# A cross-attention kernel: the last 128 columns of the next keys as 15 block products among the wide products with V

## The chip, the cores and the metric

The kernel runs on one core of a Trainium2 chip. Its time is the device time of one execution in microseconds; the figure before the change is the median of three runs, 932.97 us (932.73 to 934.45). A profile of one more execution (933.61 us) shows where that time goes.

## The reference

There are 16 batches of 100 queries with 640 channels (`x`) and a context of 722 rows with 384 channels, of which the last 4 rows are tokens (`ca`) and the first 718 the keys' rows (`enc`). Eight heads of 80 channels.

```
query = x @ Wq;  keyt = enc @ Wk;  valt = enc @ Wv
hs = mha(query, keyt, valt)                      # the main attention, over 718 rows
ca_q1 = (ca^T @ Wq_ca)[picked rows]              # the second attention:
ca_hs1 = mha(ca_q1, x, x)                        #   over x itself,
ca_hs2 = mha(ca_hs1 @ Wq, ca @ Wk_ca, ca @ Wv_ca)#   and then over the 4 tokens
out = (hs + ca_hs2) @ Wout + b_out + x
```

Everything is float32. `mha` is softmax(q k^T / sqrt(80)) v for each head.

## The kernel before

**Work of a batch.** The main loop runs over the batches `b`. In batch `b` TensorE does, in the order of the program: the scores of `b` in three groups (`scores`), two small products of the second attention (`z_ps`, `y_ps`), the values of `b` and the keys of `b + 1` block by block, alternating (`Values`, `Keys`), the last keys of `b + 1` (`last_keys`), the output projection of rows that are ready (`project`), in odd batches the queries of the next two batches (`queries`), the denominators of the softmax with a few output columns (`rests`, tile `r_ps`), and the wide products of the probabilities with V (`wides`, tile `a_ps`). Inside the loop each engine takes its instructions in the order in which they are written; nothing reorders them.

**Keys by blocks.** K^T is kept as `kT`, five chunks of 128 columns by three thirds of 240 rows. The first four chunks are made from 15 products of sums of blocks of the context (`a_form`) with sums of blocks of the weights (`wk_sb`, `weight_sums`), instead of 18 plain ones. `V_PLAN` and `K_PLAN` name for each product its PSUM bank (A to E), its number and the output block (third, half) to which the bank's content goes then. A bank carries a running sum: product after product is added to it, and after each the content is read out, the first time into an output block by an ACT copy, later by a DVE addition (`Blocks.go`). So a bank's next product has to wait until its content has been read. The fifth chunk, columns 512 to 639, is made plainly in `last_keys`: three thirds by three blocks of 128 input channels, nine products of 128 columns, weights in `wk4`, moved to `kT` by two ACT copies (L604).

**PSUM.** Eight banks in three pools: two pairs (`pair`), two single banks `psumk`, two single banks `psum1`. Score groups 0 and 2 use both pairs, group 1 the four single banks. `wides` and `rests` each take a `psum1`.

**Column halves.** In `wides` a head's 64 columns go to partitions 0 to 63 (even heads) or 64 to 127 (odd heads), so neighbouring products use different halves of the array's columns. Position `i * NH + h` counts these 48 products.

**Softmax.** The main maximum is taken on DVE (`larger`, then `Maximum`: transpose, reductions, spread, transpose back), followed by `subtract` on DVE and `exponential` on ACT for the three probability tiles `st`. The second attention has the same steps in `softmax1` (five steps of `Maximum` and the subtraction from `e1`) and `exponentials1` (L837). In batches 1 to 14 `softmax1` stands ahead of `project`, `exponentials1` ahead of `rests`. In batch 0 the first four steps stand ahead of `rests`, and the last step, the subtraction and the exponential stand at the batch's end.

**Quotients.** `divide` makes the inverse of the denominators (ACT L980, DVE L981 and L984), sends it through DRAM to `ratio` for later use by POOL (`place`), and finishes the last 128 output columns (ACT L997, DVE L999). It stands between `rests` and `wides`. `keep` copies the wide products out (ACT L1024).

Of the kernel before, what the change touches and what calls it, by code (L numbers as in the profile page):

```python
# [15 lines left out]
NH, D = 8, 80  # L16
# [123 lines left out]
K_PLAN = [V_PLAN[k] for k in (0, 1, 2, 3, 4, 6, 5, 7, 9, 11, 8, 12, 10, 13, 14)]  # L140


A_RAW = {(0, 0): 0, (0, 1): 1, (0, 2): 2, (1, 1): 3, (1, 2): 4, (2, 0): 5, (2, 1): 6}
A_REST = {(1, 0): 0, (2, 2): 1}
A_AT = {0: 0, 14: 1, 12: 2, 6: 3, 13: 4, 3: 5, 1: 6}
# [8 lines left out]
def kernel(  # L154
# [167 lines left out]
    ca_0 = small.tile([S, T, S], F32, tag="ca", name="ca_0", bufs=2)  # L322
# [164 lines left out]
    class Keys(Blocks):  # L487
# [9 lines left out]
        def product(self, at, f, first, last):  # L497
            for i in range(2):
                nc.tensor.matmul(  # L499
                    at[:, i * KT : (i + 1) * KT],  # L500
                    wk_sb[:, W_AT[f], i],
                    a_form(self.enc, f),
                    start=(first and i == 0),
                    stop=last,
                    skip_group_check=True,
                )

        def places(self, at, to):
            u, g = to
            yield (  # L510
                kT[:, : HC - 1].rearrange("p (i g) u k -> p i g u k", g=2)[:, :, g, u],
                at[:, : 2 * KT].rearrange("p (i k) -> p i k", i=2),
            )

    def enc_sums(enc):

# [71 lines left out]
    def chunk_keys(n, banks, weights, enc):  # L588
        copies = []
        for bank, thirds in zip(banks, ((0, 1), (2,))):  # L590
            for i, u in enumerate(thirds):
                for c in range(CC):
                    nc.tensor.matmul(  # L593
                        bank[:, i * KT : (i + 1) * KT],
                        weights[c],
                        a_raw(enc, u, c),
                        start=(i == 0 and c == 0),
                        stop=(c == CC - 1),
                        skip_group_check=True,
                    )  # L600
        for bank, thirds in zip(banks, ((0, 1), (2,))):
            w = len(thirds)
            copies.append(
                nc.scalar.copy(  # L604
                    kT[:, n, thirds[0] : thirds[0] + w],
                    bank[:, : w * KT].rearrange("p (u k) -> p u k", u=w),
                )
            )
        return copies

    def first_keys(enc):
        for n in range(HC - 1):
            banks = [psum(f"kT_ps_0_{n}_{k}") for k in range(2)]
            weights = [wk_sb[:, 2 * c + n % 2, n // 2] for c in range(CC)]
            copies = chunk_keys(n, banks, weights, enc)
        last_keys(0, enc)
        return copies[-1]

    def last_keys(b, enc):
        banks = pair(f"kT_ps_{b}")  # L620
        return chunk_keys(
            HC - 1,
            [banks[:, k] for k in range(2)],
            [wk4[:, c] for c in range(CC)],
            enc,
        )

# [110 lines left out]
    def load_m(b, behind=None):  # L738
        if b < 2:
            return lambda c: m_sb[c][:, b * HT : (b + 1) * HT]  # L740
        mb = small.tile([P, HC, HT], F32, tag="mb", name=f"mb_{b}", bufs=2)
# [19 lines left out]
    class Second:  # L761


        def __init__(self, b, xT, ca=None):
            self.b, self.xT = b, xT[:, b % 2]
            self.top = None

            self.ca = ca
            if ca is not None:
                return  # L770
            self.ca = small.tile([S, T, S], F32, tag="ca", name=f"ca_{b}", bufs=2)
# [167 lines left out]
    class Last:  # L939
# [36 lines left out]
        def divide(self, rests):  # L976

            b = self.b
            inverse = small.tile([P, S], F32, tag="inv", name=f"inv_{b}")
            nc.scalar.mul(inverse, rests[:, 0], qmask[:, 1:2])  # L980
            nc.vector.scalar_tensor_tensor(  # L981
                inverse, rests[:, 1], qmask[:, 0:1], inverse, ALU.mult, ALU.add
            )
# [12 lines left out]
            for to, cols in self.pieces():  # L996
                nc.scalar.mul(to[:, HC - 1], rests[:, 0, cols], qmask[:, 0:1])  # L997
            for to, cols in self.pieces():
                nc.vector.scalar_tensor_tensor(  # L999
                    to[:, HC - 1],  # L1000
# [159 lines left out]
    for c in range(HC):  # L1160
        w_ps = psum(f"w_ps_{c}")
        for cc in range(CC):
            nc.tensor.transpose(
                w_ps[:, cc * P : (cc + 1) * P], wkt_sb[:, c, cc * P : (cc + 1) * P], ident
            )
        act(
            wk_sb[:, c % 2 : 6 : 2, c // 2] if c < HC - 1 else wk4,
            w_ps[:, : CC * P].rearrange("p (a n) -> p a n", a=CC),
        )

    with tc.issue_after(summed.ins):
        for c in range(HC):
# [60 lines left out]
    for b in range(B):  # L1233
# [54 lines left out]
        if b == 0:  # L1288
# [29 lines left out]
        elif b + 1 < B:  # L1318
# [43 lines left out]
            second_next, enc_next = loads()  # L1362
            subtract(2)
            exponential(2)
            last_keys(b + 1, enc)
# [55 lines left out]
        if b == B - 2:  # L1421
            room = enc_tile("spare").rearrange("p f k -> p (f k)")
            spare.extend(room[:, i * H : (i + 1) * H] for i in range(2))
        mine.divide(rests)
        if b == B - 1:
            last.project((1,), True)
        wides = psum1(f"a_ps_{b}")[:, : 4 * S].rearrange("p (c q) -> p c q", c=4)
        for i in range(len(KC)):
            for h in range(NH):
                e = h % 2  # L1430
                nc.tensor.matmul(  # L1431
                    wides[64 * e : 64 * e + 64, h // 2],
                    slot(i, h, FIRST[e], 64),
# [66 lines left out]
```

## Time and profile before

| | |
|---|---|
| median of three runs | 932.97 us |
| the profiled execution | 933.61 us, span 931.9 us |
| TensorE busy | 923.7 us, 99% |
| DVE, ACT, POOL busy | 650.8, 375.4, 573.3 us |
| last keys (L593), all batches | 288 records at 128x240 with `wk4`, 144 products |
| wide products (L1431) | 1536 records, 768 products |

[...] In the timeline rows the first number is the start, the second the time from the first start to the last end; a matmul's recorded end lies behind the start of the next group, since products are pipelined. So lengths of TensorE's stages are best read as differences of starts. A releaser in brackets names what ended an engine's idle time.

### The profile page before, as it was taken

How to read it: one execution, taken by the hardware profiler on the slowest of the kernel's cores; microseconds unless marked ns; L12 is line 12 of the kernel's file. 1: busy time of each engine (PE TensorE's matmuls, PEld its weight loads, DVE VectorE, ACT ScalarE, POOL GpSimd, SP SyncE). 2: the span in 40 equal slices, each digit the busy share in tenths (PEclk: the TensorE clock that was granted, in tenths of full speed). 3: DMA queues.
4: the chain of work that ended last, by engine and by line, in shares of the span. 5: the costliest groups of instructions: out<-in, count | busy, mean ns of one | idle time of the engine just before them, and what ended most of it. 6: DMA issues, size and time to landing. Idle time of an engine off the chain costs nothing.

```text
span 931.9 us, 26041 instructions
## 1 busy us (share of the span) xinstructions
PE 923.7 (99%) x11183; PEld 784.3 (84%) x11183; DVE 650.8 (70%) x1087; ACT 375.4 (40%) x649; POOL 573.3 (62%) x622
## 2 busy tenths in 40 slices
PE   9999999999999999999999999999999999999998
PEld 6997879788897888988788887987889888897865
DVE  3848894886919678495955959578592876939583
ACT  2234534434334344533425434344532444434350
POOL 5649857576645865467682666756665566556444
PEclk9999999999999999999999999999999999999999
DMA  8712262051400504132131411314131050401212
GB/s 258 241 39 67 54 129 72 20 145 29 108 26 23 144 12 109 29 83 74 35 106 30 112 45 42 76 25 130 44 98 36 19 146 15 107 14 50 63 52 64
DMA packets 68667, 69.16 MB, mean 74 GB/s; under 512 B 26056, under 2 KB 62344, under 8 KB 68552
## 3 DMA queue, kind: packets, MB, share of 16 engines
q1 hardware_dynamic: 67224, 66.18, 26.9%
q8 instruction: 88, 1.44, 0.7%
q10 hardware_dynamic: 864, 0.98, 0.3%
q0 software_dynamic: 464, 0.34, 0.1%
q14 instruction: 27, 0.22, 0.1%
HBM read 61.81 MB, written 8.94 MB: 76 GB/s over the span
## 4 chain that ended last, share of the span: by engine, by line
PE 96%; DVE 2%; DMA 1%; issue 0%; ACT 0%; POOL 0%; SPq 0%; DVEq 0%; ACTq 0%
PE s_ps L643 12%; PE v_psA L468 10%; PE v_psB L468 8%; PE kT_ps L593 8%; PE k_psA L499 7%; PE q_ps L569 7%; PE a_ps L1431 7%; PE o_ps L1061 7%; PE k_psB L499 6%; PE r_ps L1413 4%; PE v_psC L468 3%; PE k_psC L499 3%; PE v_ps L409 2%; PE y_ps L782 2%; PE v_psD L468 2%; PE v_psE L468 2%
## 5 line engine op out<-in xcount | busy, mean ns | idle before, releaser
L817 POOL TENSOR_TENSOR e<-ca,g 100x800 f32<-100x800 f32 x64 | 99.4, 1564 | 156.8 <-DVE most L1263 140.4
L534 POOL TENSOR_TENSOR enc<-enc 128x240 f32<-128x240 f32 x135 | 96.5, 725 | 21.6 <-DMA enc<-in_enct 14.6
L468 PE MATMUL v_psA<-wv_sb,enc 128*120 128x320 f32 x352 | 109.6, 434 | 0.2 <-ACT st L671 0.2
L923 POOL TENSOR_TENSOR hs<-pb,vaT 128x500 f32<-128x500 f32 x64 | 73.0, 1150 | 53.7 <-DMA pb<-wide_d 51.2
L643 PE MATMUL s_ps<-qp,kT 32*120 32x100 f32 x3072 | 97.9, 263 | 0.0
L643 PEld LDWEIGHTS s_ps<-qp,kT 32*120 32x120 f32 x3072 | 95.0, 180 | 2.1 <-issue 0.2
L824 POOL TENSOR_TENSOR e<-e,e 100x800 f32<-100x800 f32 x48 | 90.6, 1887 | 3.8
L468 PE MATMUL v_psB<-wv_sb,enc 128*120 128x320 f32 x296 | 91.9, 433 | 0.0
L499 PE MATMUL k_psA<-enc,wk_sb 128*128 128x240 f32 x360 | 87.9, 367 | 1.1 <-DVE kT L439 1.0
L1274 DVE TENSOR_TENSOR most<-st 120x800 f32<-120x800 f32 x16 | 17.6, 1100 | 100.8 <-ACT st L671 100.8
L1251 DVE TENSOR_TENSOR st<-st,over 120x1600 f32<-120x1600 f32 x47 | 85.3, 1814 | 0.0
L499 PEld LDWEIGHTS k_psA<-enc,wk_sb 128*128 128x128 f32 x360 | 68.3, 190 | 18.0 <-DVE kT L439 1.3
L468 PEld LDWEIGHTS v_psA<-wv_sb,enc 128*120 128x120 f32 x352 | 63.4, 184 | 22.4 <-DVE vs L439 0.5
L1263 DVE TENSOR_TENSOR most<-most,st 120x800 f32<-120x800 f32 x64 | 65.7, 1027 | 22.8 <-ACT st L665 21.6
L1259 ACT ACTIVATE st<-st 120x1600 f32<-120x1600 f32 x48 | 73.9, 1540 | 8.2 <-DVE st L1251 7.7
L499 PE MATMUL k_psB<-enc,wk_sb 128*128 128x240 f32 x300 | 73.1, 367 | 0.1
L468 PEld LDWEIGHTS v_psB<-wv_sb,enc 128*120 128x120 f32 x296 | 54.3, 184 | 21.7 <-DVE vs L439 0.4
L1028 POOL TENSOR_TENSOR hsT<-hsT,ratio 128x500 f32<-128x500 f32 (+22 forms) x26 | 20.5, 788 | 83.0 <-DVE st L1251 74.0
L927 POOL TENSOR_TENSOR hs<-hs,hs 128x500 f32<-128x500 f32 x48 | 68.0, 1416 | 3.8
L1431 PE MATMUL a_ps<-st,vs 120*64 120x100 f32 (+1 forms) x1536 | 69.5, 250 | 0.0
L569 PE MATMUL q_ps<-xT,wq_sb 128*128 128x200 f32 x400 | 69.1, 333 | 0.0
L1431 PEld LDWEIGHTS a_ps<-st,vs 120*64 120x64 f32 (+1 forms) x1536 | 66.4, 137 | 2.7 <-issue 2.4
(166 smaller groups left out, 1854.2 us busy)
## 6 DMA issues: line engine op xcount, KB each, us to landing
pb<-p_d SPq DMA_DIRECT2D x32, 400.0 KB
enc<-in_enct SPq DMA_DIRECT2D x30, 240.0 KB
enc<-in_enct SPq DMA_DIRECT2D x15, 360.0 KB
xT<-in_xt SPq DMA_DIRECT2D x8, 500.0 KB
rest<-in_enct SPq DMA_DIRECT2D x31, 120.0 KB
xn<-in_x SPq DMA_DIRECT2D x11, 320.0 KB
wide_d<-p_d SPq DMA_DIRECT2D x16, 200.0 KB
pb<-wide_d SPq DMA_DIRECT2D x16, 200.0 KB
```

The costliest lines, as they stand in the source:

```text
L468: nc.tensor.matmul(at[0][j][:KN, : H // 2], a_form(self.enc, f)[:, j * KN : (j + 1) * KN], wv_there.get(f, wv_sb[:, W_AT[f]]), start=first ...
L499: nc.tensor.matmul(at[:, i * KT : (i + 1) * KT], wk_sb[:, W_AT[f], i], a_form(self.enc, f), start=(first and i == 0), stop=last, skip_grou ...
L534: nc.gpsimd.tensor_tensor(out, left, right, op)
L569: nc.tensor.matmul(q_ps[:, : 2 * S].rearrange("p (j s) -> p j s", j=2), wq_sb[:, c, n * P : (n + 1) * P], xT[:, :, c, :], start=(c == 0), ...
L593: nc.tensor.matmul(bank[:, i * KT : (i + 1) * KT], weights[c], a_raw(enc, u, c), start=(i == 0 and c == 0), stop=(c == CC - 1), skip_group ...
L643: nc.tensor.matmul(s_ps[bank][:n, 256 * a + lo : 256 * a + lo + rhs.shape[-1]], kT[rows, c, u, j * KN : (j + 1) * KN], rhs, start=bank not ...
L817: first = nc.gpsimd.tensor_tensor(to, self.ca[:, t, :].unsqueeze(1).to_broadcast([S, NH, S]), g[:, :, t].unsqueeze(2).to_broadcast([S, NH, ...
L824: nc.gpsimd.tensor_tensor(e, e, to, ALU.add)
L923: first = nc.gpsimd.tensor_tensor(to, pb[:, :, t], va.to_broadcast([P, HC, S]), ALU.mult)
L1251: return engine.tensor_tensor(st[i], st[i], top.over[:KN].unsqueeze(1).to_broadcast([KN, 2, ROWS]), ALU.subtract,)
L1259: nc.scalar.activation(st[i], st[i], AF.Exp, scale=SCALE)
L1431: nc.tensor.matmul(wides[64 * e : 64 * e + 64, h // 2], slot(i, h, FIRST[e], 64), st[i // 2][: KEYS[i], i % 2, h * S : (h + 1) * S], start ...
```

## The change

The fifth chunk of the keys of `b + 1` is now also made from the 15 block products, 64 columns wide, by a new class `LastKeys`. Its products are given out in eight entries of `PAIRS`, each with the position among the 48 wide products at which it is to be issued: two entries before the first, then at 12, 16, 20, 29, 37 and 45 (the last with one product). Each pair has one product for partitions 0 to 63 and one for 64 to 127. The content of a bank is read after each pair, by ACT copies (six) and DVE additions (nine); the reading of products 6 and 11 is put off until the entry at 29 has been issued. `wk4` goes; `wk_sb` gets 64 more columns per block and `weight_sums` covers them.

`divide` is split. `scale` (two or three ACT instructions) is issued at position 8 of the wide products, and the rest, on DVE and SP, after all of them, ahead of `keep` on ACT in the program. In all batches but the last, only the first four steps of `softmax1` stay where they were; the last step, the subtraction and `exponentials1` stand at the end of the batch, after `keep`. `ca` and `mb` have one buffer instead of two. In batch 0 the first two entries are issued ahead of `rests`.

```diff
+PAIRS = [
+    (0, ("D", 1, (2, 0)), ("C", 12, (0, 1))),
+    (0, ("A", 7, (2, 1)), ("B", 13, (1, 0))),
+    (12, ("A", 3, (2, 0)), ("B", 8, (2, 0))),
+    (16, ("E", 6, (1, 0)), ("C", 11, (2, 1))),
+    (20, ("A", 9, (1, 0)), ("B", 10, (2, 1))),
+    (29, ("A", 2, (0, 0)), ("B", 4, (0, 1))),
+    (37, ("A", 0, (0, 1)), ("B", 14, (0, 0))),
+    (45, ("A", 5, (1, 1))),
+]
+LATER = (6, 11)
...
-    wk_sb = const.tile([P, NF, 2, P], F32, name="wk_sb")
-    wk4 = const.tile([P, CC, P], F32, name="wk4")
+    wk_sb = const.tile([P, NF, KW], F32, name="wk_sb")
...
+    class LastKeys:
+        def __init__(self, b, enc):
+            self.enc = enc
+            self.pairs = list(PAIRS)
+            both = pair(f"kT_ps_{b}")
+            self.banks = {
+                "A": psumk(f"kT_psA_{b}")[:64],
+                "B": psumk(f"kT_psB_{b}")[64:],
+                "C": both[64:, 0],
+                "E": both[:64, 0],
+                "D": both[:64, 1],
+            }
+            self.begun, self.opened, self.kept = set(), set(), []
+        def go(self, done):
+            while self.pairs and self.pairs[0][0] <= done:
+                products = self.pairs.pop(0)[1:]
+                for bank, f, to in products:
...
+                    nc.tensor.matmul(
+                        self.banks[bank][:, :KT],
+                        wk_sb[:, W_AT[f], 2 * P :],
+                        a_form(self.enc, f),
...
+                for bank, (u, g) in reads:
+                    out = kT[64 * g : 64 * g + 64, HC - 1, u]
+                    left = self.banks[bank][:, :KT]
+                    if (u, g) in self.begun:
+                        nc.vector.tensor_tensor(out, left, out, ALU.add)
+                    else:
+                        nc.scalar.copy(out, left)
+                    self.begun.add((u, g))
...
+        def scale(self):
+            rests = self.rests
+            self.inverse = small.tile([P, S], F32, tag="inv", name=f"inv_{self.b}")
+            nc.scalar.mul(self.inverse, rests[:, 0], qmask[:, 1:2])
+            for to, cols in self.pieces():
+                nc.scalar.mul(to[:, HC - 1], rests[:, 0, cols], qmask[:, 0:1])
...
-            last_keys(b + 1, enc)
             if b + 2 < B:
                 enc_next = load_rest(b + 2, enc_next)
-            second.softmax1()
+            second.softmax1(4)
             last.project()
...
-        if 0 < b < B - 1:
-            second.exponentials1()
...
-        mine.divide(rests)
+        mine.rests = rests
         if b == B - 1:
+            mine.scale()
+            mine.divide()
             last.project((1,), True)
+        elif b:
+            rest = LastKeys(b + 1, enc)
...
                 e = h % 2
+                if b < B - 1:
+                    rest.go(i * NH + h)
+                if b < B - 1 and i * NH + h == 8:
+                    mine.scale()
...
         if b < B - 1:
+            mine.divide()
             mine.keep(wides)
...
-        if b == 0:
+        if b < B - 1:
             second.softmax1()
             second.exponentials1()
```

More of the change, by code (lines that the diff above doesn't have):

```diff
@@ L513, in places @@
             )
+    class LastKeys:
[15 more added lines that the diff above has]
+                for bank, f, to in products:
+                    last = not any(bank == p[0] for q in self.pairs for p in q[1:])
+                    nc.tensor.matmul(
+                        self.banks[bank][:, :KT],
+                        wk_sb[:, W_AT[f], 2 * P :],
+                        a_form(self.enc, f),
+                        start=bank not in self.opened,
+                        stop=last,
+                        skip_group_check=True,
+                    )
+                    self.opened.add(bank)
+                reads = [(bank, to) for bank, f, to in products if f not in LATER]
+                self.kept += [(bank, to) for bank, f, to in products if f in LATER]
+                if len(self.pairs) == 2:
+                    reads += self.kept
+                for bank, (u, g) in reads:
[6 more added lines that the diff above has]
+                    self.begun.add((u, g))
     def enc_sums(enc):
@@ L592, in chunk_keys @@
                 for c in range(CC):
[L593 to L600, printed above, removed]
+                    for lo, w in weights[c]:
+                        nc.tensor.matmul(
+                            bank[lo : lo + w.shape[-1], i * KT : (i + 1) * KT],
+                            w,
+                            a_raw(enc, u, c),
+                            start=(i == 0 and c == 0),
+                            stop=(c == CC - 1),
+                            skip_group_check=True,
+                        )
         for bank, thirds in zip(banks, ((0, 1), (2,))):
@@ L613, in first_keys @@
             banks = [psum(f"kT_ps_0_{n}_{k}") for k in range(2)]
-            weights = [wk_sb[:, 2 * c + n % 2, n // 2] for c in range(CC)]
+            weights = [
+                [(0, wk_sb[:, 2 * c + n % 2, n // 2 * P : (n // 2 + 1) * P])]
+                for c in range(CC)
+            ]
             copies = chunk_keys(n, banks, weights, enc)
@@ L623, in last_keys @@
             [banks[:, k] for k in range(2)],
-            [wk4[:, c] for c in range(CC)],
+            [[(64 * g, wk_sb[:, 2 * c + g, 2 * P :]) for g in range(2)] for c in range(CC)],
             enc,
@@ L770, in __init__ @@
                 return
-            self.ca = small.tile([S, T, S], F32, tag="ca", name=f"ca_{b}", bufs=2)
+            self.ca = small.tile([S, T, S], F32, tag="ca", name=f"ca_{b}")
             nc.sync.dma_start(
@@ L974, in parts, with divide @@
             return [(64 * k, slice(k * (H // 2), (k + 1) * (H // 2))) for k in range(2)]
[L976 to L980, printed above, removed]
+        def scale(self):
[4 more added lines that the diff above has]
+                nc.scalar.mul(to[:, HC - 1], rests[:, 0, cols], qmask[:, 0:1])
+        def divide(self):
+            b, rests, inverse = self.b, self.rests, self.inverse
             nc.vector.scalar_tensor_tensor(
@@ L1312 @@
             exponential(2)
-            last_keys(b + 1, enc)
+            rest = LastKeys(b + 1, enc)
+            rest.go(0)
             keys(m_next)
```

25 lines of the change are left out of this document (15 added, 10 removed).

## The prediction

> **What bounds the kernel now.** I read the page first (busy shares, the chain that ended last), then TensorE's timeline over one whole batch, then the ACT and DVE timelines around the place where one batch hands over to the next.
>
> ```profile
> span 931.9 us, 26041 instructions
> PE 923.7 (99%) x11183; PEld 784.3 (84%) x11183; DVE 650.8 (70%) x1087; ACT 375.4 (40%) x649; POOL 573.3 (62%) x622
> PE 96%; DVE 2%; DMA 1%; issue 0%; ACT 0%; POOL 0%; SPq 0%; DVEq 0%; ACTq 0%
> ```
>
> TensorE bounds everything: 96% of the chain is its own work. So time taken off TensorE is time gained, and any wait put on it is time lost. Batch 6, an even one without queries, looks like this on TensorE:
>
> ```profile
> 418.42 1.38 PE L593 MATMUL kT_ps<-enc,wk 128*128 128x240 f32 x6
> ...
> 422.06 5.55 PE L1061 MATMUL o_ps<-wout_sb,hsT 128*128 128x320 f32 x20
> 427.54 2.29 PE L1413 MATMUL r_ps<-st,vs 120*32 120x100 f32 x96
> 429.76 4.35 PE L1431 MATMUL a_ps<-st,vs 120*64 120x100 f32 x96
> 434.03 1.10 PE L643 MATMUL s_ps<-qp,kT 32*120 32x100 f32 x32
> ...
> 436.49 1.00 PE L643 MATMUL s_ps<-qp,kT 32*120 32x100 f32 x32
> ...
> 438.84 1.00 PE L643 MATMUL s_ps<-qp,kT 32*120 32x100 f32 x32
> ```
>
> The reader is to see that each group starts where the one before it lets go. The last keys take 422.06 - 418.42 = 3.64 us (18 records, two for each of 9 f32 products: 0.405 us a product). The wide products with V take 434.03 - 429.76 = 4.27 us for 48 products. Of the three score groups of the next batch, the third starts 438.84 - 434.03 = 4.81 us after the first. The third takes the same two bank pairs as the first, so it can't start before both ACT copies of the first have emptied them. That is the deadline on which this prediction turns.
>
> **The change, part by part.** *The products.* Nine full-width products (3.64 us) go; fifteen 64-column products come, in seven pairs and one single, of 240 moving columns each. Whether two such tiles run beside each other is read from the wide products, which alternate between the same two column halves:
>
> ```profile
> L1431 PE MATMUL a_ps<-st,vs 120*64 120x100 f32 x1024 | 50.2, 251 | 0.0
> L1431 PEld LDWEIGHTS a_ps<-st,vs 120*64 120x64 f32 x1024 | 45.3, 137 | 2.7 <-issue 2.4
> ```
>
> 48 products in 4.27 us are 24 slots of 0.178 us; a product of 100 columns alone would take 100/240 of 0.405 = 0.169 us, so two do run in the time of one. A pair of block products should then cost what one full-width product does, 0.405 us, and the eight lower-half products (one in every entry of PAIRS) give 8 x 0.405 = 3.24 us. The entries at 29, 37 and 45 stand before an upper-half product; the single at 45 has an upper wide product beside it, which makes up the slot lost at 29. TensorE's own gain is 3.64 - 3.24 = 0.40 us a batch, 5.6 us over batches 1 to 14. Bounds: 0 with 0.05 us lost at each of eight insertions, 0.40 with none.
>
> The "TensorE: Matmul & The Clock Gate" page of the Trainium skill (Part 3, "The mechanism") says that a weight load overlaps running matmuls only when the row group differs. By that rule the 30 loads of a batch, all on the same rows, would add 30 x 0.137 = 4.1 us a batch. The trace speaks against it: the 96 loads of one batch's wide products are 13.2 us by their mean and fit in 4.27 us.
>
> *What the move uncovers.* Without last keys ahead of them, the projection and the row sums start 3.64 us sooner. They need the exponentials:
>
> ```profile
> 419.21 1.54 ACT L1259 ACTIVATE st<-st 120x1600 f32<-120x1600 f32 x1
> 422.26 0.82 ACT L604 COPY kT<-kT_ps 128x480 f32<-128x480 f32 x2 [1.51 <-PE kT_ps L593]
> ```
>
> The last exponential ends at 420.75, 6.79 us before the row sums at 427.54; 3.15 us are left. Odd batches have queries ahead of the row sums and more room. So this costs nothing; the cover is 3.15 us. The second row also gives the lag from products to their reader: the copy at 422.26 starts 0.20 us after the next products did.
>
> *Batch 0* has neither projection nor queries to fill in:
>
> ```profile
> 90.32 1.38 PE L593 MATMUL kT_ps<-enc,wk 128*128 128x240 f32 x6
> ...
> 94.05 2.51 PE L1413 MATMUL r_ps<-st,vs 120*32 120x100 f32 x96
> 96.50 4.35 PE L1431 MATMUL a_ps<-st,vs 120*64 120x100 f32 x96
> 100.77 1.10 PE L643 MATMUL s_ps<-qp,kT 32*120 32x100 f32 x32
> ...
> 105.58 1.00 PE L643 MATMUL s_ps<-qp,kT 32*120 32x100 f32 x32
> ```
>
> ```profile
> 94.06 1.55 ACT L1259 ACTIVATE st<-st 120x1600 f32<-120x1600 f32 x1 [0.76 <-DVE st L1251]
> ```
>
> ```profile
> 98.05 0.98 DVE L733 COPY spread<-mx 128x800 f32<-128x800 f32 x1
> 98.95 0.31 DVE L981 SCALAR_TENSOR_TENSOR inv<-r_ps,qmask,inv 128x100 f32<-128x100 f32 x1
> ...
> 100.52 1.00 DVE L736 STREAM_TRANSPOSE over<-spread 128x800 f32<-128x800 f32 x1
> 101.55 0.99 DVE L834 TENSOR_TENSOR e<-e,over 100x800 f32<-100x800 f32 x1
> ```
>
> The last exponential ends at 95.61, so the row sums can't end sooner than now. Two pairs fit in the hole; the other six add 6 x 0.405 = 2.43 us. DVE is in the second attention's maximum until 99.03, so the first additions wait and hold the pair at 20 by about 0.5 us (an estimate; 0 to 1). Batch 0: +2.9 us.
>
> *The moved softmax.* This is the expensive part. In batches 1 to 14 the final transpose, the subtraction and the exponential of the second attention now stand behind the wide products, and on DVE behind nine additions and `divide`, which the change also moves there. ACT takes instructions in order, and the exponential stands ahead of the copies of the first scores. Batch 0 already does it so, without additions and with `divide` done early:
>
> ```profile
> 102.64 0.87 ACT L837 ACTIVATE e<-e 100x800 f32<-100x800 f32 x1 [1.26 <-DVE e L834]
> 103.49 1.55 ACT L671 COPY st<-s_ps 120x800 f32<-120x800 f32 x2
> ```
>
> From the transpose's start at 100.52 to the end of both copies at 105.04 are 4.52 us; the third score group started at 105.58, 0.54 us later. The transpose started 0.25 us before the scores did (100.77), so it must start within 0.29 us behind their start if TensorE isn't to wait. When will it start now?
>
> ```profile
> 88.70 0.65 DVE L439 TENSOR_TENSOR kT<-k_psA,kT 128x480 f32<-128x480 f32 x1
> 89.27 0.64 DVE L439 TENSOR_TENSOR kT<-k_psC,kT 128x480 f32<-128x480 f32 x1
> ```
>
> ```profile
> 430.27 0.32 DVE L981 SCALAR_TENSOR_TENSOR inv<-r_ps,qmask,inv 128x100 f32<-128x100 f32 x1 [1.73 <-ACT inv L980]
> ...
> 431.62 0.44 DVE L999 SCALAR_TENSOR_TENSOR hsT<-r_ps,qmask,hsT 128x40 f32<-128x40 f32 x2
> 438.34 0.99 DVE L1274 TENSOR_TENSOR most<-st 120x800 f32<-120x800 f32 x1 [6.29 <-ACT st L671]
> ```
>
> The last two additions read the pair at 37. Behind that pair follow five lower slots (5 x 0.178) and the single (0.405): it ends 1.30 us before the next scores start. Lag 0.20; two additions of 240 columns, each about half of the 0.57 us at which those of 480 follow each other, with some fixed part: 0.32 each (between 0.29 and 0.41). `divide` occupies DVE 1.57 us with one output piece (98.95 to 100.52), about 1.7 with two. The transpose starts at -1.30 + 0.20 + 0.64 + 1.7 = +1.24 us. That is 0.95 us too late, and TensorE waits about 1.0 us for the third score group. DVE's 6.29 us of idleness in that row is why its additions cost nothing by themselves; what costs is their place ahead of a chain with a deadline.
>
> ```profile
> 435.59 2.12 POOL L534 TENSOR_TENSOR enc<-enc 128x240 f32<-128x240 f32 x3
> ```
>
> ```profile
> 478.19 1.46 DVE L834 TENSOR_TENSOR e<-e,over 100x800 f32<-100x800 f32 x1
> ```
>
> In even batches POOL's sums run until 437.71, into the place where the subtraction will stand, and beside POOL it has taken 1.46 instead of 0.99 us. Even batches may thus wait 1.0 to 1.5 us, odd ones 1.0. I take 1.15 at all 15 handovers: 17.3 us (bounds: 0.6 with additions of 0.29 and `divide` at 1.5; 1.8 with 0.41 and POOL).
>
> *The rest.* The single-buffered `ca` and `mb` are loaded long after their last reader, and in batch 0 the wait of `ca` holds the loads of the next context on SP by some 3 us, ahead of POOL work that has room; nothing. `weight_sums` gets 64 more columns while TensorE does the first keys; nothing. Batch 0's own last keys become pairs of equal length; nothing.
>
> **Sum**, against the profiled execution's 933.6 us (span 931.9; the median of the runs, 933.0, is 0.6 lower): -5.6 + 2.9 + 17.3 = +14.6, so 948 us.
>
> **The rivals.** *No wait at the handover* ends on the other side: if the transpose can start within 0.29 us of the scores, by DVE steps 0.95 us shorter than my sum, only -5.6 + 2.9 is left: 931 us. For it speaks that batch 0 meets the deadline today by 0.54 us; against it, that at the shortest durations the sum still is 0.6 us over. *A small wait*, about 0.2 us, cancels the gain: 934. *Evictions in the way*: the banks A and B carry running sums, so a product has to wait for the reader of the one before. At 12 four ACT copies must be done in the 1.03 us of six slots, the row of L604 giving 0.41 us a copy at twice the partitions; if the stretch grows by 0.8 us a batch: 960. "TensorEngine Tiling" in the Trainium skill (Performance Considerations, PSUM Bottleneck) says the same in general: tiling makes TensorE faster, not the emptying of PSUM; the 0.82 us for two copies here against fifteen evictions bear out that the emptying grows. *Pairs don't overlap*: each pair takes 0.81 us, 7 x 0.405 = 2.8 us a batch more, about 990; the slots of 0.178 us speak against it.
>
> **How the numbers follow.** Wait at the handover as summed 0.66 (940 to 957), evictions in the way 0.12 (955 to 968), no wait 0.12 (929 to 932), a small wait 0.06 (932 to 937), pairs apart 0.04. The range 937 to 960 leaves out the no-wait and the small-wait case, the pairs apart and the upper half of the eviction case. A difference under 0.2% (1.9 us) can't be told from none; faster 0.13, same 0.05, slower 0.82.
>
> **What would show it.** In TensorE's timeline the wide stretch with its block products lasts 7.5 us and pairs start within 10 ns of each other. A gap of 1.0 to 1.5 us stands ahead of the third score group from batch 1 on, put down to ACT's copies of `st`; on ACT the exponential ends some 5 us behind the start of the scores. Row sums follow the projection without a wait, except in batch 0. I am wrong if that gap isn't there, if DVE reaches the transpose before the scores start, or if gaps stand inside the wide stretch.

## The result and the profile after

The changed kernel takes 957.97 us (median of four runs, 957.5 to 959.17) against 933.24 us (932.73 to 934.45) for the kernel before, measured beside it: a ratio of 1.0262 with the interval 1.0248 to 1.0277. It is slower by 24.7 us, where 948 (14.6 us more) was forecast. The profiled execution took 958.21 us, its span is 956.5 us; the spans differ by 956.5 - 931.9 = 24.6 us.

From the page of the changed kernel: span, busy time by engine, and the chain that ended last.

```profile
span 956.5 us, 26623 instructions
PE 938.2 (98%) x11381; PEld 778.0 (81%) x11381; DVE 697.4 (73%) x1222; ACT 391.0 (41%) x709; POOL 570.4 (60%) x622
PE 83%; DVE 9%; ACT 2%; issue 2%; POOL 2%; DMA 2%; SPq 0%; POOLq 0%; DVEq 0%; ACTq 0%
```

TensorE's own work is no longer 96% of the chain but 83%, and DVE holds 9%: the chain now leaves TensorE and passes through DVE and back, in most batches. That TensorE is still "98% busy" says little here, for the ends of matmuls in the records overlap the waits of the next ones.

TensorE's timeline of the changed kernel, batch 6 (start, duration, instruction, records in the row; a bracket is idle time and what ended it):

```profile
436.13 0.63 PE L550 MATMUL kT_ps<-enc,wk_sb 128*64 128x240 f32 x4
436.58 0.37 PE L550 MATMUL kT_psA<-enc,wk_sb 128*64 128x240 f32 x1
436.59 0.37 PE L550 MATMUL kT_psB<-enc,wk_sb 128*64 128x240 f32 x1
...
438.02 0.57 PE L550 MATMUL kT_psA<-enc,wk_sb 128*64 128x240 f32 x2
438.33 0.42 PE L550 MATMUL kT_psB<-enc,wk_sb 128*64 128x240 f32 x1
...
441.17 0.42 PE L550 MATMUL kT_psB<-enc,wk_sb 128*64 128x240 f32 x1
...
443.60 0.42 PE L550 MATMUL kT_psA<-enc,wk_sb 128*64 128x240 f32 x1
...
444.32 1.10 PE L704 MATMUL s_ps<-qp,kT 32*120 32x100 f32 x32
...
449.69 0.45 PE L704 MATMUL s_ps<-qp,kT 32*120 32x100 f32 x4 [0.38 <-ACT st L732]
450.41 0.98 PE L704 MATMUL s_ps<-qp,kT 32*120 32x100 f32 x26 [0.27 <-ACT st L732]
452.96 0.75 PE L905 MATMUL z_ps<-y,e 100*32 100x33 f32 x64
```

Three things are to be seen. The stretch of the wide products with their block products, up to the next scores, lasts 444.32 - 436.13 = 8.19 us, where last keys and wide products together took 3.64 + 4.27 = 7.91 before: the stretch got longer by 0.28 us, not shorter by 0.40. Pairs do start 10 ns apart (436.58 and 436.59), but the pair at 12 doesn't: A at 438.02, B 0.31 us later. And the third score group starts at 449.69 with four records, stops again, and goes on at 450.41; 4.81 us after the first it would have been 449.13. From the first scores to the second attention's sums are 452.96 - 444.32 = 8.64 us here; the undisturbed length is 7.28 us (the same difference in nearly every batch before). At the 15 handovers, where one batch's wide products give way to the next one's scores, it is now 8.31 to 8.75 us, 8.41 in the median.

DVE and ACT of the changed kernel in the same stretch:

```profile
438.63 0.40 DVE L567 TENSOR_TENSOR kT<-kT_psA,kT 64x240 f32<-64x240 f32 x1 [3.69 <-PE kT_psA L550]
...
440.70 0.41 DVE L567 TENSOR_TENSOR kT<-kT_psB,kT 64x240 f32<-64x240 f32 x1
...
442.27 0.84 DVE L567 TENSOR_TENSOR kT<-kT_ps,kT 64x240 f32<-64x240 f32 x2
443.14 0.40 DVE L567 TENSOR_TENSOR kT<-kT_psA,kT 64x240 f32<-64x240 f32 x1
443.57 0.41 DVE L567 TENSOR_TENSOR kT<-kT_psB,kT 64x240 f32<-64x240 f32 x1
444.02 0.32 DVE L1048 SCALAR_TENSOR_TENSOR inv<-r_ps,qmask,inv 128x100 f32<-128x100 f32 x1
...
445.72 1.00 DVE L797 STREAM_TRANSPOSE over<-spread 128x800 f32<-128x800 f32 x1
446.75 1.26 DVE L895 TENSOR_TENSOR e<-e,over 100x800 f32<-100x800 f32 x1
```

```profile
436.80 0.72 ACT L569 COPY kT<-kT_ps 64x240 f32<-64x240 f32 x2 [6.02 <-PE kT_ps L550]
437.54 0.35 ACT L569 COPY kT<-kT_psA 64x240 f32<-64x240 f32 x1
437.92 0.36 ACT L569 COPY kT<-kT_psB 64x240 f32<-64x240 f32 x1
...
448.05 0.87 ACT L898 ACTIVATE e<-e 100x800 f32<-100x800 f32 x1 [2.87 <-DVE e L895]
448.83 1.53 ACT L732 COPY st<-s_ps 120x800 f32<-120x800 f32 x2
```

ACT lies idle 2.87 us ahead of the exponential, with the copies that TensorE needs queued behind it. The copies end at 448.83 + 1.53 = 450.36, and TensorE goes on at 450.41; its four records from 449.69 on stand behind the first of the two copies. Bank B's first copy is the last of four that ACT makes in a row; it ends at 438.28, and B's next product starts at 438.33.

Over all batches, by the same differences of starts:

| part | predicted | measured |
|---|---|---|
| stretch of wide and block products, 14 batches | 14 x -0.40 = -5.6 | 14 x +0.28 = +3.9 |
| batch 0 (first scores of batch 1 at 103.66 instead of 100.77) | +2.9 | +2.9 |
| 15 handovers (score groups 134.2 us in all instead of 117.1) | +17.3 | +17.1 |
| batch 15 (its wide products' stretch 6.00 instead of 4.64) | 0 | +1.4 |
| sum | +14.6 | +25.3 |

The spans differ by 24.6; 0.7 us of the sum isn't assigned.

### The profile page after: what moved, and what is told of

It is laid out like the page before. It is cut to its first block, busy times and chain, and to the rows that moved or that the text cites. A ratio compares the mean times of both kernels' runs of the same rounds, so it can differ in the third digit from the quotient of the medians.

```text
span 956.5 us, 26623 instructions
## 1 busy us (share of the span) xinstructions
PE 938.2 (98%) x11381; PEld 778.0 (81%) x11381; DVE 697.4 (73%) x1222; ACT 391.0 (41%) x709; POOL 570.4 (60%) x622
## 3 DMA queue, kind: packets, MB, share of 16 engines
q8 instruction: 89, 1.46, 0.6%
## 4 chain that ended last, share of the span: by engine, by line
PE 83%; DVE 9%; ACT 2%; issue 2%; POOL 2%; DMA 2%; SPq 0%; POOLq 0%; DVEq 0%; ACTq 0%
PE v_psA L482 9%; PE v_psB L482 8%; PE k_psA L513 7%; PE q_ps L626 7%; PE o_ps L1126 6%; PE s_ps L704 6%; PE k_psB L513 6%; PE a_ps L1507 5%; PE r_ps L1481 3%; PE v_psC L482 3%; PE k_psC L513 2%; DVE kT L567 2%; PE v_ps L423 2%; PE kT_psA L550 2%; ACT st L732 2%
## 5 line engine op out<-in xcount | busy, mean ns | idle before, releaser
L704 PE MATMUL s_ps<-qp,kT 32*120 32x100 f32 x3072 | 108.2, 265 | 7.0 <-ACT st L732 6.2
L704 PEld LDWEIGHTS s_ps<-qp,kT 32*120 32x120 f32 x3072 | 100.4, 179 | 16.4 <-ACT st L732 14.3
L1507 PE MATMUL a_ps<-st,vs 120*64 120x100 f32 (+1 forms) x1536 | 107.1, 250 | 0.0
L1507 PEld LDWEIGHTS a_ps<-st,vs 120*64 120x64 f32 (+1 forms) x1536 | 95.3, 136 | 5.4 <-issue 0.6
L567 DVE TENSOR_TENSOR kT<-kT_psA,kT 64x240 f32<-64x240 f32 x45 | 18.0, 400 | 103.1 <-PE kT_psA L550 102.6
L513 PEld LDWEIGHTS k_psA<-enc,wk_sb 128*128 128x128 f32 x360 | 68.2, 190 | 17.7 <-DVE kT L453 0.9
L626 PEld LDWEIGHTS q_ps<-xT,wq_sb 128*128 128x128 f32 x400 | 67.9, 190 | 0.6
```

Source lines behind the costliest of these rows:

```text
L513: nc.tensor.matmul(at[:, i * KT : (i + 1) * KT], wk_sb[:, W_AT[f], i * P : (i + 1) * P], a_form(self.enc, f), start=(first and i == 0), st ...
L626: nc.tensor.matmul(q_ps[:, : 2 * S].rearrange("p (j s) -> p j s", j=2), wq_sb[:, c, n * P : (n + 1) * P], xT[:, :, c, :], start=(c == 0), ...
L704: nc.tensor.matmul(s_ps[bank][:n, 256 * a + lo : 256 * a + lo + rhs.shape[-1]], kT[rows, c, u, j * KN : (j + 1) * KN], rhs, start=bank not ...
L1507: nc.tensor.matmul(wides[64 * e : 64 * e + 64, h // 2], slot(i, h, FIRST[e], 64), st[i // 2][: KEYS[i], i % 2, h * S : (h + 1) * S], start ...
```

## The experiments

In the main theory the loss has two places that don't depend on each other: the wait at the handover (DVE late, ACT's exponential ahead of copies that TensorE needs) and a stretch in which block products wait for readers. The rivals were that the late order alone costs the time, that DVE's lateness itself does, and that the block products are slow by themselves. All ratios are against the kernel before.

**The softmax early again.**

```diff
-            second.softmax1(4)
+            second.softmax1()
             last.project()
...
+        if 0 < b < B - 1:
+            second.exponentials1()
         rests = psum1(f"r_ps_{b}")[:, : 2 * S].rearrange("p (e q) -> p e q", e=2)
...
-        if b < B - 1:
+        if b == 0:
             second.softmax1()
             second.exponentials1()
```

> The changed kernel with the second attention's last steps put back: all of softmax1 ahead of the projection and its exponential ahead of the row sums in batches 1 to 14; block products and the late quotients stay. Theory (the wait ahead of the third score group comes from transpose, subtraction and exponential queued behind additions and quotients): the three score groups take 7.28 us again in batches 2 to 15, 14 x 1.13 us go, about 942 us. Rival (the wait comes from the bank pair, the ACT copies or the additions of the block products themselves): the score groups stay at 8.4 us and the time at 958.

Measured: 949.43 us, ratio 1.0158 (1.0140 to 1.0176). The scores are back at 7.28 us in batches 2 to 15, so the wait at the handover goes as expected; but the time missed 942 by 7.4 us. The stretch became 9.0 us in the seven even batches (9.14 in batch 6) and stayed at 8.19 in the odd ones. TensorE and ACT of this kernel in batch 6:

```profile
433.93 0.63 PE L550 MATMUL kT_ps<-enc,wk_sb 128*64 128x240 f32 x4
...
436.70 0.62 PE L550 MATMUL kT_psA<-enc,wk_sb 128*64 128x240 f32 x2 [0.71 <-ACT kT L569]
...
443.07 1.10 PE L704 MATMUL s_ps<-qp,kT 32*120 32x100 f32 x32
```

```profile
434.80 0.88 ACT L898 ACTIVATE e<-e 100x800 f32<-100x800 f32 x1 [6.21 <-DVE e L895]
435.58 0.70 ACT L569 COPY kT<-kT_ps 64x240 f32<-64x240 f32 x2
```

The exponential that was moved forward now stands on ACT ahead of the first block copies, and DVE's subtraction lets it start only at 434.80. The first copies begin 435.58 - 433.93 = 1.65 us after the block products instead of 436.80 - 436.13 = 0.67 us, and the pair at 12 waits 0.71 us for a copy. Over the seven batches the longer stretch comes to 5.8 us of the miss; the rest isn't assigned. So the late order had a use that the prediction didn't see: in even batches, which have no queries as cover, it kept ACT clear for the block copies.

**Only the late order, without block products** (in the kernel before):

```diff
-            second.softmax1()
+            second.softmax1(4)
...
-        if 0 < b < B - 1:
-            second.exponentials1()
...
-        mine.divide(rests)
         if b == B - 1:
+            mine.divide(rests)
             last.project((1,), True)
...
         if b < B - 1:
+            mine.divide(rests)
             mine.keep(wides)
...
-        if b == 0:
+        if b < B - 1:
             second.softmax1()
             second.exponentials1()
```

> The kernel before with only the late order of the change: quotients written behind the wide products, last steps of the second attention at the batch's end; last keys plain as before, no block products. Theory (the late order costs only because nine additions stand ahead of it on DVE): quotients run as soon as the row sums are there, the transpose starts before the scores do, no wait, 932 to 935 us. Rival (the late order itself costs, by ACT's exponential ahead of the copies of the first scores): 0.5 to 1.0 us at 14 handovers, 940 to 947 us.

Measured: 933.83 us, ratio 0.9996 (0.9987 to 1.0005), score groups of 7.28 us (7.33 in one batch, 7.67 in the last, which took 7.94 before). DVE and TensorE in batch 6:

```profile
432.21 1.00 DVE L736 STREAM_TRANSPOSE over<-spread 128x800 f32<-128x800 f32 x1
```

```profile
434.27 1.10 PE L643 MATMUL s_ps<-qp,kT 32*120 32x100 f32 x32
```

The late order alone costs nothing: the transpose starts 2.06 us before the scores. It takes the additions ahead of it on DVE to push it past its deadline.

**The reciprocal and its trip last.** `divide` is cut in two: what reads the row sums' bank stays, all of it ahead of the transpose; the reciprocal, the way through DRAM and the shuffle go behind softmax and exponential.

```diff
+        def invert(self):
+            b, inverse = self.b, self.inverse
             nc.vector.reciprocal(inverse, inverse)
...
             second.softmax1()
             second.exponentials1()
+            mine.invert()
```

> The changed kernel with the reciprocal, its trip through DRAM and the shuffle put behind the second attention's last steps; only the DVE steps that read the row sums stay ahead of them. Theory: the transpose starts 1.0 us sooner, the wait of 1.13 us ahead of the third score group shrinks to 0.1 to 0.4 us, about 944 us. Rival (the wait does not hang on DVE's queue): 958 us.

Measured: 942.09 us, ratio 1.0091 (1.0074 to 1.0108); the stretch is unchanged at 8.19 us, the scores take 7.28 to 7.64. TensorE and ACT in batch 6:

```profile
437.77 1.10 PE L704 MATMUL s_ps<-qp,kT 32*120 32x100 f32 x32
...
442.58 1.00 PE L704 MATMUL s_ps<-qp,kT 32*120 32x100 f32 x32
```

```profile
440.12 0.87 ACT L898 ACTIVATE e<-e 100x800 f32<-100x800 f32 x1 [1.48 <-DVE e L895]
440.90 1.53 ACT L732 COPY st<-s_ps 120x800 f32<-120x800 f32 x2
```

The exponential starts 2.35 us behind the scores instead of 448.05 - 444.32 = 3.73, both copies end 4.66 us behind them, and the third group starts at its 4.81 us. At 14 of the 15 handovers the transpose now starts 0.16 to 0.29 us behind the scores, just within the 0.29 us that the prediction worked out as its deadline, and at ten of them the scores take 7.28 us.

**Only ACT's order**: DVE as late as in the changed kernel, but the exponential stands behind the copies of the first scores.

```diff
         st.append(scores(b, 0, tiles))
-        if b == 0:
-            now.exponentials1()
+        now.exponentials1()
...
             second.softmax1()
-            second.exponentials1()
```

> The changed kernel with one thing moved: the second attention's exponential stands on ACT behind the copies of the first scores of the next batch instead of ahead of them. DVE's order, quotients and block products stay. Theory (TensorE waits only because ACT, in order, can't copy the first scores before the exponential, and that waits for DVE): score groups of 7.28 us again, 15 x 1.13 us go, about 941 us. Rival (the lateness of DVE itself delays the batch, the order on ACT only shows it): 950 to 958 us.

Measured: 942.03 us, ratio 1.0080 (1.0065 to 1.0095). The scores take 7.28 us everywhere. TensorE and ACT in batch 6:

```profile
437.60 1.10 PE L704 MATMUL s_ps<-qp,kT 32*120 32x100 f32 x32
...
442.41 1.00 PE L704 MATMUL s_ps<-qp,kT 32*120 32x100 f32 x32
```

```profile
440.32 1.55 ACT L732 COPY st<-s_ps 120x800 f32<-120x800 f32 x2 [1.86 <-PE s_ps L704]
441.76 0.88 ACT L898 ACTIVATE e<-e 100x800 f32<-100x800 f32 x1
```

The rival that DVE's lateness costs by itself falls: its steps are as late as they were, and one instruction moved on ACT gives back 957.97 - 942.03 = 15.9 us. The wait needs both, a late subtraction and the copies queued behind what waits for it; taking away either one is enough. The score groups alone shrink by 134.2 - 116.5 = 17.7 us; 1.8 us come back in the second attention's sums right behind them, which take 13.4 us in all instead of 11.6.

**Few readings.** Each bank is read once, by its last reader; ten of the fifteen readings, with them all nine additions, are left out, so the last 128 key columns aren't the reference's.

```diff
-                reads = [(bank, to) for bank, f, to in products if f not in LATER]
+                reads = [(bank, to) for bank, f, to in products if f in (1, 5, 14)]
```

> The changed kernel with ten of the fifteen readings of the block products' banks left out (all but the last one of each bank), so no product waits for a reader of the one before; the last 128 columns of the keys are therefore not the reference's. Theory (the stretch of wide and block products is 8.19 instead of 7.51 us because banks A and B wait for their readers): the stretch is about 7.5 us. Rival (TensorE itself can't run 240-column block products among 100-column wide ones without loss): it stays at 8.0 to 8.2 us. With the nine additions gone DVE is early and the wait at the handover goes in both; total about 931 us by the theory, 941 by the rival.

Measured: 929.50 us, ratio 0.9953 (0.9937 to 0.9969). TensorE in batch 6:

```profile
425.15 0.63 PE L550 MATMUL kT_ps<-enc,wk_sb 128*64 128x240 f32 x4
...
427.05 0.37 PE L550 MATMUL kT_psA<-enc,wk_sb 128*64 128x240 f32 x1
427.05 0.37 PE L550 MATMUL kT_psB<-enc,wk_sb 128*64 128x240 f32 x1
...
429.65 0.42 PE L550 MATMUL kT_psB<-enc,wk_sb 128*64 128x240 f32 x1
...
432.69 1.10 PE L704 MATMUL s_ps<-qp,kT 32*120 32x100 f32 x32
```

The stretch is 432.69 - 425.15 = 7.54 us, the prediction's 7.51. The same products in the same places cost what their slots cost as soon as nothing reads the banks in between. So the 0.65 us from here to 8.19 come with the readings; that it is the wait for them and not the reading itself is shown by the next kernel, which makes all fifteen in 7.57 us. Without the additions the score groups take 7.28 us too, as expected.

The weight-load rule weighed in the prediction (the Trainium skill, "TensorE: Matmul & The Clock Gate", Part 3, "The mechanism"), taken by row groups alone, would have made this stretch 4.1 us longer (the prediction's estimate); the 7.54 us don't show it. The same section allows an early load into a background weight buffer as well; no run here tells which of the two lets the loads overlap.

**Readings spaced and shared.** On top of the kernel with the reciprocal last: three entries two positions earlier, two a position later, the first copies of C and B on DVE, the reading of product 11 no longer put off and that of product 6 made one entry earlier.

```diff
-    (12, ("A", 3, (2, 0)), ("B", 8, (2, 0))),
-    (16, ("E", 6, (1, 0)), ("C", 11, (2, 1))),
-    (20, ("A", 9, (1, 0)), ("B", 10, (2, 1))),
-    (29, ("A", 2, (0, 0)), ("B", 4, (0, 1))),
-    (37, ("A", 0, (0, 1)), ("B", 14, (0, 0))),
+    (10, ("A", 3, (2, 0)), ("B", 8, (2, 0))),
+    (14, ("E", 6, (1, 0)), ("C", 11, (2, 1))),
+    (18, ("A", 9, (1, 0)), ("B", 10, (2, 1))),
+    (30, ("A", 2, (0, 0)), ("B", 4, (0, 1))),
+    (38, ("A", 0, (0, 1)), ("B", 14, (0, 0))),
...
-LATER = (6, 11)
+LATER = (6,)
...
-                if len(self.pairs) == 2:
+                if len(self.pairs) == 3:
...
+                    elif len(self.begun) in (1, 3):
+                        nc.vector.tensor_copy(out, left)
```

> The kernel with the inverse last, and the block products given more room for their readers: entries at 0, 0, 10, 14, 18, 30, 38, 45, the first copies of the second and fourth output block on DVE instead of ACT, product 11 read at once, product 6 behind the entry at 18. Theory (only the waits for readers lengthen the stretch): 8.19 us become 7.5 to 7.6, 14 x 0.63 us go from 942, about 933 us, with batch 0 still 2.9 us longer than before. Rival (the readers are as late as before, DVE being as full as before): 8.0 to 8.2 us, 940 to 942 us.

Measured: 938.77 us, ratio 1.0059 (1.0045 to 1.0074). The stretch fell to 7.57 us with every reading made (7.76 and 7.79 in two of the 14 batches), as expected; but from its first scores to the next batch's, batch 0 is 6.76 us longer than before, where the kernel with the reciprocal last was 2.98 longer. That is 3.8 of the 5.8 us by which 933 was missed. TensorE and DVE in batch 0:

```profile
101.59 1.06 PE L550 MATMUL kT_psA<-enc,wk_sb 128*64 128x240 f32 x2 [3.19 <-DVE kT L567]
```

```profile
95.65 0.41 DVE L569 COPY kT<-kT_psB 64x240 f32<-64x240 f32 x1
95.99 1.00 DVE L769 STREAM_TRANSPOSE turned<-e 128x800 f32<-128x800 f32 x1
...
100.12 0.98 DVE L796 COPY spread<-mx 128x800 f32<-128x800 f32 x1
101.13 0.40 DVE L567 TENSOR_TENSOR kT<-kT_psA,kT 64x240 f32<-64x240 f32 x1
```

In batch 0 the two copies stand on DVE ahead of the second attention's maximum, which starts behind them; the first addition comes at 101.13, and TensorE waits 3.19 us for it. It is the cost that the prediction gave batch 0 (DVE busy with the maximum when the additions are due), made larger.

**Batch 0 as before**: the last keys of batch 1 are made plainly. In this kernel the raw weights have been overwritten by weight sums by then, so the last key columns of batch 1 aren't the reference's; the next kernel keeps those weights in the room of another tile and takes the last batch's quotients at once.

```diff
-            rest = LastKeys(b + 1, enc)
-            rest.go(0)
+            last_keys(b + 1, enc)
...
-                if b < B - 1:
+                if 0 < b < B - 1:
                     rest.go(i * NH + h)
```

> As the one before, and batch 0 makes the last keys of batch 1 plainly where the kernel before did, in the hole ahead of its row sums. Theory (batch 0 pays 2.9 us because six of eight entries come out of a hole in which plain ones were free): 2.9 us less than the kernel with spaced entries, about 930 us, faster than before by 0.3%. Rival (batch 0 is bound by DVE, not by its products): no more than 1 us less.

> As the kernel with spaced entries and plain last keys in batch 0, with the raw weights of the last 128 columns kept beside their sums (in the room that the output weights take from batch 1 on), so that all keys are the reference's, and with the quotients of the last batch made at once as in the kernel before. Theory (what is left against the kernel before is the pairs' gain, 14 x 0.35 us, less some 0.1 us a batch at the handover and up to 1 us in batch 0): 930 to 931 us, faster than before by 0.2 to 0.4%. Rival (the gain is eaten at other places, as the 0.16% of the kernel before this one suggests): 932 to 933 us.

Measured: 932.43 us, ratio 0.9984 (0.9975 to 0.9993), and 932.86, ratio 0.9992 (0.9983 to 1.0001). Plain products in batch 0 took 6.3 us off the kernel with spaced readings, so the rival that batch 0 is bound by DVE falls; but both miss their forecasts of 930 and 930 to 931 us by some 2 us, and the second one's time is the one that its rival gave. (The two figures of the first forecast don't agree: 2.9 us less than 938.77 would be 935.9.) From TensorE's timeline of the first, and from the waits of the second (time in total, how often, the longest):

```profile
99.13 2.80 PE L1513 MATMUL a_ps<-st,vs 120*64 120x100 f32 x60 [0.98 <-issue]
```

```profile
PE o_ps L1159 <- POOL hsT L1105: 1.4, 1, 1.4
```

In the first, batch 0 has a gap of 0.98 us in its wide products that the profile puts down to nothing; it stays open. In the second a projection in the last batch waits 1.4 us for a quotient on POOL; this wait, 0.8 to 1.4 us, is there in all four kernels with the reciprocal last and in no other. And at four handovers (to batches 3, 7, 9 and 11) the scores still take 7.78 to 7.85 us. The reciprocal last comes with a price of its own.

**All of it, with ACT's order instead of the reciprocal last**: the exponential behind the copies, the readings spaced and shared, batch 0 plain with its raw weights kept, quotients as in the changed kernel. (The entries, as in the kernel with spaced readings, are left out here.)

```diff
-            rest = LastKeys(b + 1, enc)
-            rest.go(0)
+            last_keys(b + 1, enc)
...
+            act(wk4, w_ps[:, : CC * P].rearrange("p (a n) -> p a n", a=CC))
...
-        if b == 0:
-            now.exponentials1()
+        now.exponentials1()
```

> The moved exponential, the spaced entries and the plain last keys of batch 0 together, quotients as in the changed kernel. Theory: nothing but the pairs' gain of 0.35 us in batches 1 to 14 is left, 928 to 930 us, faster than before by 0.4 to 0.5%. Rival (something at the end of the kernel or in the odd batches takes it, as in the kernel with the raw weights kept): 932 to 933 us.

Measured: 930.41 us, ratio 0.9962 (0.9950 to 0.9974): faster than both kernels. TensorE and ACT in batch 6:

```profile
425.15 0.63 PE L551 MATMUL kT_ps<-enc,wk_sb 128*64 128x240 f32 x4
...
432.72 1.10 PE L707 MATMUL s_ps<-qp,kT 32*120 32x100 f32 x32
...
437.53 1.00 PE L707 MATMUL s_ps<-qp,kT 32*120 32x100 f32 x32
```

```profile
435.44 1.55 ACT L735 COPY st<-s_ps 120x800 f32<-120x800 f32 x2 [1.86 <-PE s_ps L707]
```

The stretch is 432.72 - 425.15 = 7.57 us and the third group starts after 4.81 us. Over 14 batches the stretch saves 14 x (7.91 - 7.57) = 4.8 us; some of it comes back in the second attention's sums, which take 1.0 to 1.2 us instead of 0.68 in four of the batches and 1.97 instead of 0.93 in the last. These sums take 13.9 us in all instead of 11.6 before. The kernel with only ACT's order changed has the same (13.4), those with the exponential ahead of the copies don't (11.1 to 11.9): it goes with the moved exponential; how wasn't studied. With the readers out of the way the block products give nearly what the prediction had for them.

## Why the prediction was right, and where it was wrong

- *The sign and its main cause held; that the sum came so close is luck in part.* The handover was summed at 17.3 us and measures 17.1. By its steps, in batch 6: `divide` from its first DVE step to the transpose 445.72 - 444.02 = 1.70 us (taken: 1.7); the transpose starts 445.72 - 444.32 = 1.40 us behind the scores (1.24). What was added for POOL didn't come: the subtraction takes 0.99 us at 12 of the 15 handovers (1.08, 1.11 and, in batch 6, 1.26 at the others; up to 1.46 had been reckoned with), and handovers out of odd batches wait as long (1.20 us in the mean) as those out of even ones (1.17). The later transpose made up for it. (The terms named for the bounds 0.6 and 1.8 give 0.69 and 1.60.) That both an order on ACT and a chain on DVE are needed is shown by the kernel with only ACT's order changed and the one with only the late order.
- *DVE's additions were mis-sized.* The two on the path were taken at 0.32 us each; they take 0.40 and 0.41 and follow each other at 443.57 - 443.14 = 0.43 us. At the handover this cost only the 0.16 us that the transpose came later; in the stretch it adds to the waits of the next point.
- *The step that failed is "TensorE's own gain is 3.64 - 3.24 = 0.40 us a batch".* The slots are right: without intermediate readings the stretch is 7.54 us. But its bounds, 0 to 0.40, hold no term for the readers, only 0.05 us lost at each insertion; by the prediction's own sign, a stretch of 7.5 us without gaps, this part was wrong. With a single bank for a running sum, a product can't start before the reader of the one before is done. Four ACT copies in a row (0.35 us each, one every 0.37) are done at 438.28, and the pair at 12 wanted to start at 438.02; behind it the second products at 29 and 37 and the single one start 0.06 to 0.08 us after DVE's addition has let their bank go. The prediction had the figures for the first of these waits: four copies at 0.41 us are 1.64, against its 1.03 us for the six slots (6 x 0.178 is 1.07). This was the rival *evictions in the way*, with the place it named (12) and about its price: it was put at 0.8 us a batch, and 8.19 - 7.51 = 0.68 us was measured. It is no alternative to the wait at the handover but comes on top of it, and the forecast gave it a chance of 0.12 instead of a term in the sum: 14 x 0.68 = 9.5 us, nearly the whole error of 10. The Trainium skill ("TensorEngine Tiling", Performance Considerations, PSUM Bottleneck) says that tiling does not speed up the emptying of PSUM; the 7.54 us without and the 8.19 us with the readings agree.
- *Batch 0*: +2.9 predicted and measured, but by two errors that cancel. The row for the start of its wide products:

```profile
95.95 1.25 PE L1507 MATMUL a_ps<-st,vs 120*64 120x100 f32 x24
```

The six entries cost what was said: with few readings the stretch of batch 0 is 6.72 us, 2.45 more than the 4.27 before (2.43 predicted). With the readings it is 103.66 - 95.95 = 7.71, so the late additions cost 0.99 us and not 0.5. But the row sums end sooner than before, which the prediction had ruled out: the last exponential ends at 95.07 instead of 95.61, and the wide products start at 95.95 instead of 96.50. Most of these 0.55 us come from DVE, where a subtraction ahead of that exponential takes 1.78 us instead of 2.25; why isn't shown.

- *The cover of the exponentials held.* In batches from 1 on the row sums follow the projection without a wait.
- *The tail was left out.* In batch 15 the projection waits 1.6 us for DVE's last quotients, 0.3 before; +1.4 us for the stretch, which the prediction put at nothing. The chain that ended last runs there from batch 14's inverse, which DVE makes behind the additions (from 902.78 on), through DRAM (back at 910.36) to POOL, the second attention of batch 15 and DVE. Whether that is the whole cause is open: with few readings there are no additions, and this stretch takes 5.81 us all the same; in the last kernel it takes 4.65.
- *Pairs do overlap*, so that rival is out. *No wait* and *a small wait* at the handover didn't come in the changed kernel; the kernels with only the late order and with only ACT's order changed show what no wait takes.

## What to carry to other kernels

When work is tucked into a stretch of a busy engine, cost its readers as their own queue: for each bank the time from a product's end to its reader's end, against the time until the next product into that bank; a chance for "the readers may be late" is no substitute for that sum. On an engine that takes instructions in order, look at what is queued behind each one that waits: here moving one exponential behind the copies gave back 15.9 us without any engine doing less, though 1.8 us of what the scores gained went to the sums behind them. And before an order is undone, ask what else it keeps clear: the early softmax removed one wait and stood in the way of the block copies instead.

## What the runs showed of the hardware that was not expected

- Two column halves run side by side until one of them waits. After the 0.31 us of the pair at 12 the halves stay out of step (the next block products of A and B start at 439.59 and 439.88, those after at 440.87 and 441.17, so 0.3 us apart still), though in the kernel with few readings they start together there (427.05, and 428.55 and 428.56). Counted from the start of the stretch and against that kernel, bank B's products are 0.30 us late at 12, 0.34 at 20, 0.54 at 29 and 0.53 at 37, the single one 0.61, and the end 0.65. So nearly half of the loss arises at 12, behind the fourth ACT copy, and is carried on; some 0.2 us come at 29, where B starts at 441.17 and DVE's addition ended at 441.11.
- Half the columns didn't halve an addition on DVE: those of 64x240 follow each other every 0.43 us, those of 128x480 every 0.57. If the difference of 0.14 us were the price of 240 columns, 0.43 - 0.14 = 0.29 us would be fixed (an estimate from these two). The recorded lengths, 0.40 and 0.65 us, would give 0.15 us fixed instead: the small additions start after the recorded end of the one before, the large ones before it. Why wasn't studied.
- The brackets of the timeline understate such waits. Ahead of the third score group in batch 6 stand 0.38 and 0.27 us, 0.65 together, while by the starts the scores take 8.64 - 7.28 = 1.36 us longer, since the recorded ends of matmuls reach into the wait (the row of 448.77 before it, for one, ends at 449.31, where the third group was due at 449.13). The difference of starts is the one to use.
